# Convolution: image blocks folded about their middle, a transform in 64-row halves, and a last inverse step in 64x32 tiles

## The chip, the cores and the metric

The kernel runs on one core of a Trainium2 chip. A core has five engines: TensorE (PE) multiplies matrices, with a separate step that loads the stationary matrix (PEld); VectorE (DVE), ScalarE (ACT) and GpSimd (POOL) work element by element; SyncE (SP) only issues transfers. PE writes to PSUM, [...]results of PE are copied ("evicted") to SBUF by ACT or DVE. DMA engines move data between HBM and SBUF. Each engine works through its own queue in order. The metric is the device time of one launch in microseconds; smaller is better.

## The reference

The input is `x`, four images of 512x512 with 16 channels, fp32. Layer 0 adds to `x` a long 2-d convolution of its group-normalized form, with a filter given as a ratio of two polynomials, evaluated by FFT at twice the size. Layer 1 adds a 3x3 cosine-similarity convolution of the result, again normalized first. Cut to what matters here:

```python
H = jnp.fft.rfft2(h_truncated, s=(2 * l1, 2 * l2))
H_full = h0 + H[0]
X = jnp.fft.rfft2(x, s=(2 * l1, 2 * l2), axes=(-3, -2))
Y = jnp.einsum('...hwi,ijhw->...hwj', X, H_full)
y = jnp.fft.irfft2(Y, s=(2 * l1, 2 * l2), axes=(-3, -2))
return y[..., :l1, :l2, :]
...
x = x + _L0_conv_ref(_gn(x), L0_conv_h0, L0_conv_numerators, L0_conv_denumerator)
x = x + _L1_conv_ref(_gn(x), L1_conv_kernel, L1_conv_bias, L1_conv_radius)
```

The change is confined to layer 0.

## The kernel before

The program has four stages, one after the other. `filter_phase` makes the filter's transform along the width and stores its taps in `g_d`. `forward_phase` normalizes the images and transforms them along the width into `x_d`. `conv_phase` convolves along the height, one width frequency (a "row") at a time, into `y_d`. `last_phase` transforms back along the width (to `yw_d`) and does layer 1.

The work is written with a tile framework. A tile is taken from a pool with a fixed number of buffers, and waits for a free one. The framework orders the instructions of each engine itself when the program is built: what stands earlier in the program goes first, unless by its own estimate it isn't ready and something later is. So the order in the queues is fixed at build time, and is not always that of the text. `InOrder` forces the order only in `filter_phase`.

**forward_phase** runs over 4 images and 4 blocks of 128 image rows (`ht`). It loads four 1 MB pieces `xt` of a block (L626), folds the width about its middle into sums on DVE (`xu`, L632) and differences on POOL (L634), transposes both by PE through two PSUM tiles `pt` (L641), scales on the way out with ACT and DVE into `xw`, and multiplies with a fixed cosine and sine matrix `fwd` (L663). Each result `pf` (four PSUM tiles) is evicted to `xo`, the cosine half by DVE (L671), the sine half by ACT (L673), and `xo` is stored to `x_d` (L675).

**conv_phase** handles 513 rows: frequencies 1 to 511, and two planes for the two purely real ones. Height 512 is cut in 64 positions by 8 shifts; along the 64 a length-128 transform is taken. The work on a row is spread over several steps of the loop `step(n)`, each of which treats four rows at different depths, in four parts k = 0 to 3:

- `load_x`, `load_g`, `load_xe` are issued by SP at the start of a step.
- `turn_x` makes this row's transform matrix `dfs_n` out of a constant and its phase, one ACT and one DVE instruction.
- `x_part` (row n+2, at k=0, after `over_q`): one 128x128 by 128x256 matmul for each image (L766) into PSUM tiles `px` of two images each; each tile is evicted to `xe`.
- `x_late` (row n+2) on POOL: four products `xu` (L787), one product and one sum `xl` (L788, L789), and two stores to the scratch `xf_d`, from which `load_xe` fetches shifted copies a step later. `half_shift` copies the two remaining shifts inside SBUF by ACT (L798): one from `xe`, one from `xl`.
- `g_part` (row n+1): four matmuls of 64x128 pairs a part (L818, into `pg`), evicted to `gh` in two copies.
- `mix` (row n): 32 matmuls a part in four 128x32 column tiles (L834, into `pm`), evicted to `yf` in one copy.
- `over_q` (row n-1): four transposes a part (L855, into `pz`); ACT copies half of `pz` (`zq`, L862) and DVE works the rest through in five instructions (L863 to L867), using `pz` as scratch to the end. At the end POOL makes `zd` and folds `z` (L871, L873).
- `over_g` (row n-2, at k=2): eight matmuls of 128x64 by 128x256 in two column tiles (L892, into one tile `py`), one eviction to `yo`, one store to `y_d` by POOL's queue (L903).

The PSUM tiles of the loop are three `pg`, two `pm`, and three of the tag `full`, which `px`, `pz` and `py` share. The eviction helper `evict` counts: every third call goes to DVE (L716), the others to ACT (L718). A row makes 15 such calls. In the queues as built, ACT copies `xl` (second L798) ahead of the evictions `yf` and `gh` of k=2, though in the text it stands behind those of k=3.

A matmul in fp32 shows as two records in the profile, a transpose as one.

Of the kernel before, what the change touches and what calls it, by code (L numbers as in the profile page):

```python
# [69 lines left out]
def constants():  # L70
# [79 lines left out]
    f, sb = np.arange(F), np.arange(S)  # L150
    d = np.zeros((2, S, F, 2))
    co, si = turn(np.outer(sb + 31.5, f), F)
    d[0, :, :, 0], d[0, :, :, 1] = co, -si
    d[1, :, :, 0], d[1, :, :, 1] = si, co
    c["dfs"] = np.stack([d, np.stack([d[..., 1], -d[..., 0]], -1)], 2).reshape(P, -1)
# [5 lines left out]
    ig = np.zeros((32, 2, 2, 4, 2, 2, 2, 16))  # L161
    for s0 in range(4):
        for cx in range(2):
            for c2 in range(2):
                n = gg[:, None] * s0 + 4 * gg[:, None] * s1[None, :] + 32 * (cx + c2)
                co, si = turn(n, F)
                for b2 in range(2):
                    ig[:, cx, b2, s0, c2, 0, b2, :] = co / F
                    ig[:, cx, b2, s0, c2, 1, b2, :] = si / F
# [427 lines left out]
def forward_phase(tc, cst, x, mvs, x_d):  # L597
    nc = tc.nc
    with ExitStack() as ctx:
        cp = ctx.enter_context(tc.tile_pool(name="x_const", bufs=1))  # L600
        xp = ctx.enter_context(tc.tile_pool(name="x_in", bufs=8))
        sm = ctx.enter_context(tc.tile_pool(name="x_small", bufs=B))
        up = ctx.enter_context(tc.tile_pool(name="x_u", bufs=4))
        tp = ctx.enter_context(tc.tile_pool(name="x_t", bufs=2))
# [12 lines left out]

        for b in range(B):
            scale, bias = norm[b]
            twice = sm.tile([P, 8], F32, name="twice")  # L620
            nc.vector.tensor_add(twice, bias, bias)
            for ht in range(4):
                xt = []
                for w in range(4):
                    t = xp.tile([P, P, C], F32, name="xt")
                    nc.sync.dma_start(out=t, in_=x[b, ht * P : (ht + 1) * P, w * P : (w + 1) * P, :])  # L626
                    xt.append(t)

                su = []
                for w in range(2):  # L630
                    u = up.tile([P, P, C], F32, name="xu")
                    nc.vector.tensor_add(u, xt[w], xt[3 - w][:, ::-1, :])  # L632
                    su.append(u)
                    nc.gpsimd.tensor_sub(xt[w], xt[w], xt[3 - w][:, ::-1, :])  # L634
                halves = su + xt[:2]
                xw = tp.tile([P, 4, C, P], F32, name="xw")
                for i4 in range(4):
                    for w in range(4):
                        pt = ps_x.tile([P, 4, P], F32, name="pt")
                        for i in range(4):  # L640
                            nc.tensor.transpose(pt[:, i], halves[w][:, :, 4 * i4 + i], ident)  # L641
                        for i2 in range(2):
                            g = 2 * i4 + i2
                            dst = xw[:, w, 2 * g : 2 * g + 2, :]
                            src = pt[:, 2 * i2 : 2 * i2 + 2, :]
                            if i2 == 0 and w < 2:
                                nc.scalar.activation(dst, src, AF.Identity,
                                                     scale=scale[:, g : g + 1], bias=twice[:, g : g + 1])
                            elif i2 == 0:
                                nc.scalar.activation(dst, src, AF.Identity, scale=scale[:, g : g + 1])  # L650
                            elif w < 2:
                                nc.vector.tensor_scalar(dst, src, scale[:, g : g + 1],
                                                        twice[:, g : g + 1], ALU.mult, ALU.add)
                            else:
                                nc.vector.tensor_scalar(dst, src, scale[:, g : g + 1], None, ALU.mult)
                for rc in range(4):
                    o = op.tile([P, 2, 16, 8, C], F32, name="xo")
                    for c in range(2):
                        col = (2 * rc + c) * P
                        for i4 in range(4):  # L660
                            pf = ps_f.tile([P, 4, 16, 8], F32, name="pf")
                            for w in range(2):
                                nc.tensor.matmul(  # L663
                                    pf.rearrange("p i s t -> p (i s t)"), fwd[:, w, col : col + P],
                                    xw[:, 2 * c + w, 4 * i4 : 4 * i4 + 4, :].rearrange("p i h -> p (i h)"),
                                    start=(w == 0), stop=(w == 1),
                                )
                            dst = o[:, c, :, :, 4 * i4 : 4 * i4 + 4]
                            src = pf.rearrange("p i s t -> p s t i")[:, :, ::-1, :]
                            if c == 0:  # L670
                                nc.vector.tensor_copy(dst, src)  # L671
                            else:
                                nc.scalar.copy(dst, src)  # L673
                    for c in range(2):
                        nc.sync.dma_start(  # L675
                            out=dram(x_d[rc], None, c * X_ROW // 2 + (16 * ht * B + b) * C * 8,
                                     [B * C * 8, 16], [1, C * 8]),
                            in_=o[:, c].rearrange("p s t i -> p s (t i)"),
                        )
# [5 lines left out]
def conv_phase(tc, cst, g_d, x_d, y_d):  # L685
    nc = tc.nc
    with ExitStack() as ctx:
# [11 lines left out]
        dfs = load_const(nc, cp, cst, "dfs").rearrange("p (v n) -> p v n", v=2)  # L699
        dg = load_const(nc, cp, cst, "dg")  # L700
        ident = load_const(nc, cp, cst, "ident")
        ig = load_const(nc, cp, cst, "ig").rearrange("p (s c n) -> p s c n", s=4, c=2)
# [29 lines left out]
        def load_x(n):  # L732
            rc, r, plane = rows[n]
            x = io.tile([P, B, 8 * C], F32, name="x")
            t, w = x.rearrange("p b x -> p (b x)"), B * 8 * C
            if plane is None:
                nc.sync.dma_start(out=t, in_=dram(x_d[rc], r, 0, [w, P], [1, w]))
            else:
                nc.gpsimd.memset(t[S:], 0.0)
                nc.sync.dma_start(out=t[:S], in_=dram(x_d[rc], r, plane * S * w, [w, S], [1, w]))  # L740
            state["x", n] = x

        def turn_x(n):
# [8 lines left out]
            t = xlp.tile([P, 2 * F], F32, name="turn")  # L752
            nc.scalar.activation(t, dfs[:, 1], AF.Identity, scale=own[:, 1, at])
            m = xlp.tile([P, 2 * F], F32, name="dfs_n", bufs=2)
            nc.vector.scalar_tensor_tensor(m, dfs[:, 0], own[:, 0, at], t, ALU.mult, ALU.add)
            state["dfs", n] = m

        def x_part(n, b):

            if b == 0:  # L760

                state["xe", n] = xep.tile([P, 8, F, 2, 2, 2], F32, name="xe")
            if b % 2 == 0:
                state["px"] = ps_f.tile([P, 2, F, 2], F32, name="px", tag="full")
            px = state["px"]
            nc.tensor.matmul(px[:, b % 2].rearrange("p f c -> p (f c)"), state["x", n][:, b],  # L766
                             state["dfs", n], start=True, stop=True)
            if b % 2:
                evict(state["xe", n][:, 0, :, b // 2], px.rearrange("p k f c -> p f c k"))
            if b == B - 1:  # L770
                del state["x", n], state["dfs", n]

        def x_late(n):

            xe = state["xe", n][:, 0]
            fl = xe.rearrange("p f h c k -> p f (h c k)")
# [6 lines left out]
            xl = xlp.tile([P, F, 2, 2, 2], F32, name="xl")  # L783
            u = xlp.tile([P, F, 2, 2, 2], F32, name="xu")
            for c in range(2):
                for h in range(2):
                    nc.gpsimd.tensor_mul(u[:, :, h, c], xe[:, :, h, 1 - c], bc(late[:, 1 + c], 2, [P, F, 2]))  # L787
            nc.gpsimd.tensor_mul(xl.rearrange("p f h c k -> p f (h c k)"), fl, bc(late[:, 0], 2, [P, F, 8]))  # L788
            nc.gpsimd.tensor_add(xl.rearrange("p f h c k -> p (f h c k)"),  # L789
                                 xl.rearrange("p f h c k -> p (f h c k)"),  # L790
                                 u.rearrange("p f h c k -> p (f h c k)"))
            store(1, xl.rearrange("p f h c k -> p f (h c k)"))
            state["xl"] = xl

        def half_shift(n, half):

            dst, src = ((slice(0, 64), state["xe", n][64:, 0]), (slice(64, P), state["xl"][:64]))[half]
            nc.scalar.copy(state["xe", n][dst, 4].rearrange("p f h c k -> p (f h c k)"),  # L798
                           src.rearrange("p f h c k -> p (f h c k)"))
# [27 lines left out]
        def mix(n, g):  # L827
# [10 lines left out]
            if g == 7:  # L838

                state["y", n] = yp.tile([P, 16, 32, 4], F32, name="yf")  # L840
# [585 lines left out]
```

## Time and profile before

| | |
|---|---|
| median of 3 runs | 18402.83 us (18401.31 to 18431.59) |
| profiled execution, span from first to last instruction | 18387.3 us |
| mean granted TensorE clock | 0.957 |
| stage 1, `filter_phase` | about 0 to 5350 us |
| stage 2, `forward_phase` | about 5350 to 6460 us |
| stage 3, `conv_phase` | about 6460 to 15550 us |
| stage 4, `last_phase` | from about 15550 us |

Shares of the whole span: PE 90%, PEld 66%, DVE 63%, ACT 53%, POOL 57%. These are means over stages with different limits, so they say little about any one of them. In the groups of instructions, a line gives the source line, the engine, output and inputs, how often, then busy time and mean length, then the idle time of the engine just before and what ended it. PE's busy time is modelled: matmuls are pipelined, so groups of them overlap, and the distance from one group's start to the next is the better measure. "issue" as a releaser means that the engine waited for nothing that the profile shows.

### The profile page before, as it was taken

The numbers are of one execution on the slowest core, as the hardware profiler recorded it, in microseconds if no ns is written. First come the engines' busy times: TensorE is split into PE (matmuls) and PEld (weight loads), VectorE is DVE, ScalarE is ACT, GpSimd is POOL, SyncE is SP. The second block draws the span as 40 slices with busy tenths as digits, with TensorE's granted clock in tenths as the row PEclk, the third lists the DMA queues.
The fourth block names the chain that finished last, engine by engine and source line by source line (L and its number), as shares of the span: only waits on it lengthen the run. The fifth ranks groups of instructions, "written<-read, shape, count | busy, mean of one in ns | idle before, by whom it ended". The sixth has DMA issues, their size and how long they took to land. (4 is left out here: it accounts for less than half of the span.)

```text
span 18387.3 us, 530668 instructions
## 1 busy us (share of the span) xinstructions
PE 16516.6 (90%) x224908; PEld 12124.1 (66%) x224908; DVE 11547.2 (63%) x24155; ACT 9712.8 (53%) x18895; POOL 10465.0 (57%) x10653
## 2 busy tenths in 40 slices
PE   7899999999989988889888898888888887988898
PEld 4555555555544467777777777777777776877787
DVE  8988888888843345555555555555555554247887
ACT  5456666666632245555555555555555554106788
POOL 6456666666621066666666666666666664026776
PEclk8899999999999999999999999999999999998999
DMA  3665555555576588888888888888888887795431
GB/s 103 199 180 164 161 161 162 162 154 161 159 228 189 163 309 320 319 323 323 323 322 323 323 327 321 326 323 325 319 320 324 324 321 285 257 327 195 160 129 69
DMA packets 2918820, 4543.01 MB, mean 247 GB/s; under 512 B 117634, under 2 KB 2086492, under 8 KB 2809566
## 3 DMA queue, kind: packets, MB, share of 16 engines
q1 hardware_dynamic: 2686254, 3768.92, 60.5%
q0 software_dynamic: 174896, 605.89, 8.6%
q10 hardware_dynamic: 55296, 134.24, 2.2%
q8 instruction: 1772, 29.03, 0.6%
q14 instruction: 602, 4.93, 0.1%
HBM read 3031.24 MB, written 1477.31 MB: 245 GB/s over the span
## 5 line engine op out<-in xcount | busy, mean ns | idle before, releaser
L818 PE MATMUL pg<-c_dg,g 64*128 64x128 f32 x32832 | 2834.1, 291 | 336.6 <-ACT gh L718 172.3
L834 PE MATMUL pm<-xe,gh 128*32 128x64 f32 x131328 | 2395.9, 222 | 568.5 <-issue 326.8
L834 PEld LDWEIGHTS pm<-xe,gh 128*32 128x32 f32 x131328 | 2011.5, 110 | 1167.8 <-issue 980.5
L818 PEld LDWEIGHTS pg<-c_dg,g 64*128 64x128 f32 x32832 | 2284.3, 190 | 670.2 <-issue 256.1
L863 DVE TENSOR_TENSOR z<-zq,pz 128x256 f32<-128x256 f32 x2052 | 860.5, 419 | 2647.8 <-ACT zq L862 2567.5
L398 PE MATMUL pg<-c_dinv,sp 128*128 128x256 f32 x8192 | 2179.2, 414 | 223.9 <-ACT st L403 209.9
L398 PEld LDWEIGHTS pg<-c_dinv,sp 128*128 128x128 f32 x8192 | 1627.3, 204 | 915.5 <-ACT st L403 301.1
L716 DVE COPY gh<-pg 128x512 f32<-128x512 f32 x2046 | 1409.0, 689 | 1248.4 <-PE pg L818 1244.3
L378 POOL TENSOR_TENSOR x<-ab,ab 128x512 f32<-128x512 f32 x1024 | 1505.1, 1470 | 1039.3 <-ACT ab L361 993.9
L443 PE MATMUL pt<-ev_in,c_todd 128*128 128x512 f32 x4096 | 1992.3, 613 | 52.0 <-DMA ev_in<-g_d 26.6
L787 POOL TENSOR_TENSOR xu<-xe,c_late 128x256 f32<-128x256 f32 x2052 | 1390.9, 703 | 863.2 <-ACT xe L718 836.9
L376 DVE RECIPROCAL dn<-dn 128x256 f32<-128x256 f32 x1024 | 1781.1, 1739 | 0.0
L718 ACT COPY yf<-pm 128x512 f32<-128x512 f32 x2046 | 1210.2, 591 | 925.3 <-PE pm L834 910.9
L403 ACT COPY st<-pg 128x256 f32<-128x256 f32 x2048 | 1075.1, 625 | 1129.3 <-PE pg L398 724.4
L798 ACT COPY xe<-xl 64x1024 f32<-64x1024 f32 x513 | 538.4, 1050 | 1883.8 <-POOL xl L789 1883.8
L718 ACT COPY gh<-pg 128x512 f32<-128x512 f32 x2058 | 1199.9, 583 | 395.6 <-PE pg L818 386.7
L855 PE MATMUL pz<-c_ident,yf 128*128 128x128 f32 x8208 | 1371.6, 290 | 29.8 <-issue 15.0
L361 ACT COPY ab<-pab 128x512 f32<-128x512 f32 x2048 | 1121.6, 601 | 518.2 <-PE pab L352 282.0
L443 PEld LDWEIGHTS pt<-ev_in,c_todd 128*128 128x128 f32 x4096 | 810.0, 199 | 708.9 <-issue 531.9
L382 POOL TENSOR_TENSOR m<-m 128x256 f32<-128x256 f32 x1024 | 753.9, 736 | 885.8 <-DVE m L375 884.7
L789 POOL TENSOR_TENSOR xl<-xl,xu 128x1024 f32<-128x1024 f32 x513 | 1209.3, 2357 | 40.2
L1269 PE MATMUL pc<-l_band,xn 128*128 128x160 f32 (+2 forms) x6144 | 1079.4, 334 | 51.0 <-DVE e_o L1324 50.8
(205 smaller groups left out, 31650.4 us busy)
## 6 DMA issues: line engine op xcount, KB each, us to landing
xe<-xf_d SPq DMA_DIRECT2D x1026, 1536.0 KB, 10.1
g<-g_d SPq DMA_DIRECT2D x511, 1024.0 KB, 9.8
g_d<-st SPq DMA_DIRECT2D x64, 4096.0 KB, 25.7
ev_in<-g_d SPq DMA_DIRECT2D x1024, 256.0 KB, 4.8
g_d<-ot SPq DMA_DIRECT2D x1024, 256.0 KB, 2.6
xf_d<-xe POOLq DMA_DIRECT2D x513, 448.0 KB, 8.4
xf_d<-xl POOLq DMA_DIRECT2D x513, 448.0 KB, 5.4
x_d<-xo SPq DMA_DIRECT2D x128, 1024.0 KB, 5.1
```

The lines of the kernel that those rows point to most:

```text
L361: nc.scalar.copy(w["ab"][n], pp[n])
L376: nc.vector.reciprocal(w["dn"], w["dn"])
L378: nc.gpsimd.tensor_mul(w["x"], b, a[:, :, ::-1])
L398: nc.tensor.matmul(pg[:, k].rearrange("p a x -> p (a x)"), w["sp"][:, k, c, :], dinv[:, 2 * kp + k, c, :], start=(c == 0), stop=(c == 1),)
L443: nc.tensor.matmul(pt, todd[:, c, kc, hh * P : hh * P + P], ev[:, kc, c], start=(kc == 0), stop=(kc == 1),)
L716: nc.vector.tensor_copy(dst, src)
L718: nc.scalar.copy(dst, src)
L787: nc.gpsimd.tensor_mul(u[:, :, h, c], xe[:, :, h, 1 - c], bc(late[:, 1 + c], 2, [P, F, 2]))
L789: nc.gpsimd.tensor_add(xl.rearrange("p f h c k -> p (f h c k)"), xl.rearrange("p f h c k -> p (f h c k)"), u.rearrange("p f h c k -> p (f ...
L818: nc.tensor.matmul(pg[c][:, j % 4], g[half, j], dg[half], start=True, stop=True)
L834: nc.tensor.matmul(pm[32 * q : 32 * q + 32, g % 8], gh[:, f].rearrange("p c j -> p (c j)"), xe[:, :, f].rearrange("p t h c k -> p t (h c k ...
L855: nc.tensor.transpose(pz[:, t % 4].rearrange("p v q x -> p (v q x)"), y[:, at].rearrange("p g x -> p (g x)"), ident)
```

## The change

Three parts of the transform move.

**Folding the height.** In `forward_phase` a block of rows is now treated with its mirror image (`ht` with `3 - ht`). Both are loaded, folded in width, transposed and multiplied as before, the cosine part (`c = 0`) ahead of the sine part. The result of the mirrored block, read in reverse, is then added to and subtracted from that of the first: ACT copies one PSUM tile to `xa`, DVE adds and subtracts the other. The pools are recut: `x_in` 8 to 6 buffers, `x_u` 4 to 3, `x_t` 2 of 32 KB to 5 of 16 KB, and a new `x_a` with 4.

**The transform of a row.** Since sums and differences about the middle need only cosines or only sines, `x_part` multiplies two 64-row halves with a fixed matrix `dfs`, eight matmuls of 64x128 into two PSUM tiles, one for the real, one for the imaginary part. It no longer needs the row's phase, and is called ahead of `over_q`. The order of the elements in `xe`, `xl` and `yf` changes, and `xu` takes two products where it took four.

**The last inverse step.** The phase goes into the matrix of `over_g` instead (`turn_ig` in place of `turn_x`, with equal shapes). `over_g` does its sum in 16 matmuls of 64x32 by 64x256 into two tiles `py`, evicted by two calls to `evict`, so that a row has 16 calls. The store to `y_d` has runs of 1 KB where it had 2 KB; `last_phase` reads it in the new order in pieces of the same size.

```diff
-        xp = ctx.enter_context(tc.tile_pool(name="x_in", bufs=8))
+        xp = ctx.enter_context(tc.tile_pool(name="x_in", bufs=6))
...
+        def transform(xw, c, rc, i4):
+
+            col = (2 * rc + c) * P
+            pf = ps_f.tile([P, 4, 16, 8], F32, name="pf")
+            for w in range(2):
+                nc.tensor.matmul(
+                    pf.rearrange("p i s t -> p (i s t)"), fwd[:, w, col : col + P],
+                    xw[:, w, 4 * i4 : 4 * i4 + 4, :].rearrange("p i h -> p (i h)"),
+                    start=(w == 0), stop=(w == 1),
+                )
+            return pf.rearrange("p i s t -> p s t i")[:, :, ::-1, :]
...
+            for ht in range(2):
+                near, far = folded(b, ht), folded(b, 3 - ht)
+                for c in range(2):
+                    both = [turned(h[c], scale, (twice, None)[c]) for h in (near, far)]
+                    for rc in range(4):
+
+                        sums = [op.tile([P, 16, 8, C], F32, name=f"xo{k}") for k in range(2)]
                         for i4 in range(4):
...
+                            pa, pb = (transform(xw, c, rc, i4) for xw in both)
+                            pb = pb[:, ::-1]
+                            a = ap.tile([P, 16, 8, 4], F32, name="xa")
+                            nc.scalar.copy(a, pa)
+                            i = slice(4 * i4, 4 * i4 + 4)
+                            nc.vector.tensor_add(sums[0][:, :, :, i], a, pb)
+                            nc.vector.tensor_sub(sums[1][:, :, :, i], a, pb)
...
-            if b == 0:
-
-                state["xe", n] = xep.tile([P, 8, F, 2, 2, 2], F32, name="xe")
-            if b % 2 == 0:
-                state["px"] = ps_f.tile([P, 2, F, 2], F32, name="px", tag="full")
-            px = state["px"]
-            nc.tensor.matmul(px[:, b % 2].rearrange("p f c -> p (f c)"), state["x", n][:, b],
-                             state["dfs", n], start=True, stop=True)
-            if b % 2:
-                evict(state["xe", n][:, 0, :, b // 2], px.rearrange("p k f c -> p f c k"))
...
+            state["xe", n] = xep.tile([P, 8, F, B, 2], F32, name="xe")
+            px = [ps_f.tile([P, B, F], F32, name=f"px{c}", tag="full") for c in range(2)]
+            for b in range(B):
+                for c in range(2):
+                    half = slice(64 * c, 64 * c + 64)
+                    nc.tensor.matmul(px[c][:, b], state["x", n][half, b], dfs[half], start=True, stop=True)
+            for c in range(2):
+                evict(state["xe", n][:, 0, :, :, c], px[c].rearrange("p b f -> p f b"))
...
             for c in range(2):
-                for h in range(2):
-                    nc.gpsimd.tensor_mul(u[:, :, h, c], xe[:, :, h, 1 - c], bc(late[:, 1 + c], 2, [P, F, 2]))
...
+                nc.gpsimd.tensor_mul(u[:, :, :, c], xe[:, :, :, 1 - c], bc(late[:, 1 + c], 2, [P, F, B]))
...
-                state["py"] = ps_f.tile([P, 2, 2, 8, C], F32, name="py", tag="full")
...
+                state["py"] = [ps_f.tile([P, 2, 8, C], F32, name=f"py{h}", tag="full") for h in range(2)]
+            z, d, m = state["z", n], state["zd", n], state["ig", n]
+            c2 = k
+            for s0 in range(4):
...
-                nc.tensor.matmul(
-                    py[64 * half : 64 * half + 64, odd], ig[:, s0, c2],
-                    zs.rearrange("p (t h) j -> p h t j", h=2),
-                    start=(c2 == 0), stop=(c2 == 1),
-                )
...
+                for half in range(2):
+                    q = slice(64 * half, 64 * half + 64)
+                    nc.tensor.matmul(
+                        state["py"][half][32 * s0 : 32 * s0 + 32], m[q, s0, c2],
+                        zs[q].rearrange("p (t h) j -> p h t j", h=2), start=(c2 == 0), stop=(c2 == 1),
+                    )
...
-            evict(yo.rearrange("p (x j t) -> p x j t", x=4, j=C), py.rearrange("p o h t j -> p (o h) j t"))
...
+            for half in range(2):
+                evict(yo[:, half].rearrange("p (h j t) -> p h j t", h=2, j=C),
+                      state["py"][half].rearrange("p h t j -> p h j t"))
...
-                nc.gpsimd.dma_start(out=dram(y_d[rc], r, 0, [4 * P, P], [1, 4 * P]), in_=yo)
...
+                nc.gpsimd.dma_start(out=dram(y_d[rc], r, 0, [w, P], [P * w, 2], [1, w]), in_=yo)
...
+                if row(2) and k == 0:
+                    x_part(n + 2)
                 if row(-1):
                     for t in range(4):
                         over_q(n - 1, 4 * k + t)
                 if row(2) and k == 0:
-                    for m in range(B):
-                        x_part(n + 2, m)
                     x_late(n + 2)
                 if row(2) and k >= 2:
                     half_shift(n + 2, k - 2)
-                if row(3) and k == 2:
-                    turn_x(n + 3)
+                if row(-1) and k == 2:
+                    turn_ig(n - 1)
                 if row(-2) and k == 2:
-                    for m in range(4):
+                    for m in range(2):
                         over_g(n - 2, m)
```

## The prediction

> **What bounds the kernel now.** I read the page's slices first, then the busy times by stage, the waits of each engine in the longest stage, and the timeline of single rows there. Columns after the length: busy time of PE, PEld, DVE, ACT, POOL, then clock, DMA share, GB/s.
>
> ```profile
> 5378.00:6460.00 1082.00, 1026.27 (x3072) 511.55 (x3071) 398.72 (x543) 279.42 (x512) 152.48 (x36) 0.98 0.60 181
> 6600.00:15600.00 9000.00, 7994.17 (x182467) 6399.25 (x182456) 4877.85 (x13211) 4717.39 (x8610) 5696.92 (x5572) 0.98 0.86 321
> ```
>
> The first is the forward stage (PE busy 95%), the second the row loop of `conv_phase`. Its 513 rows start 17.64 us apart on average (first `px` matmul at 6466.1, last at 15499.2, over 512). No engine is full, so the loop is bound by waits:
>
> ```profile
> ACT xe L798 <- POOL xl L789: 1854.4, 504, 6.5
> ```
> ```profile
> PE pm L834 <- issue: 319.5, 321, 3.2
> PE pg L818 <- ACT gh L718: 160.3, 187, 3.7
> PE pg L818 <- issue: 157.3, 99, 3.7
> ```
>
> In nearly every row ACT stands 3.7 us in front of POOL's last `xl`. One row in order of time, PE, then POOL, then ACT:
>
> ```profile
> 12011.22 1.89 PE L766 MATMUL px<-dfs_n,x 128*128 128x256 f32 x8
> 12013.05 1.10 PE L834 MATMUL pm<-xe,gh 128*32 128x64 f32 x64
> 12022.74 0.42 PE L834 MATMUL pm<-xe,gh 128*32 128x64 f32 x14 [1.41 <-issue]
> 12023.10 1.16 PE L818 MATMUL pg<-c_dg,g 64*128 64x128 f32 x16
> 12028.13 1.89 PE L766 MATMUL px<-dfs_n,x 128*128 128x256 f32 x8
> ```
> ```profile
> 12012.95 1.36 POOL L787 TENSOR_TENSOR xu<-xe,c_late 128x256 f32<-128x256 f32 x2 [1.92 <-ACT xe L718]
> 12018.37 2.37 POOL L789 TENSOR_TENSOR xl<-xl,xu 128x1024 f32<-128x1024 f32 x1
> ```
> ```profile
> 12020.77 1.05 ACT L798 COPY xe<-xl 64x1024 f32<-64x1024 f32 x1 [3.74 <-POOL xl L789]
> 12021.84 0.58 ACT L718 COPY yf<-pm 128x512 f32<-128x512 f32 x1
> 12022.32 0.59 ACT L718 COPY gh<-pg 128x512 f32<-128x512 f32 x1
> ```
>
> The loop that sets the row: `px` starts at 12011.22; its first half is evicted; POOL does four `xu`, a store and two `xl`, to 12020.74 (9.5 us after `px`); ACT, which stood waiting with the k=2 evictions queued behind, copies `xl`, then evicts `yf` and `gh`; only then has PE a bank for the `pg` of k=3 (12023.10, 2.33 after the copy began); 5.03 us later comes the next `px`. Sum 16.9. Of 454 rows measured in the trace a tenth take under 16.90 us, half under 17.15. PE's own groups, start to start, are 4 x 1.03 (`pm`) + 3 x 1.09 + 1.08 + 0.42 (`pg`) + 4 x 0.58 (`pz`) + 1.83 (`px`) + 1.87 (`py`) = 14.9, so 2.0 us of each row is PE waiting. A long wait has a second price:
>
> ```profile
> 10014.94 0.60 PE L818 MATMUL pg<-c_dg,g 64*128 64x128 f32 x6 [2.96 <-issue]
> 10016.17 1.98 PE L892 MATMUL py<-z,c_ig 128*64 128x256 f32 x8
> ```
> ```profile
> 10015.00:10020.00 5.00, 5.00 (x57) 2.92 (x59) 2.18 (x6) 2.71 (x5) 0.57 (x1) 0.66 0.94 379
> ```
>
> After that pause the clock fell and the `py` group took 3.40 us instead of 1.87. Counting PE's pauses between 7000 and 15000 us: a half-rate spell followed 8 of 103 pauses of 1.5 to 2.0 us, 31 of 60 of 2.0 to 2.5, 19 of 27 of 2.5 to 3.0, and 10 of 12 of 3.0 to 3.5. There were 73 spells in 454 rows.
>
> [...]the spells in this trace are 3.41 us at 0.5[...]. [...]queue q8 moved 1772 packets, 29.03 MB, which is 16 KB each, and PE's pauses put down to "issue" fall where a block ends. Fetches are 3.3 us apart at the closest.
>
> **The change, part by part** (a row of the loop unless said).
>
> *x_part.* 4 matmuls of 128x256 (8 records) become 8 of 64x128 (16 records), exactly the form of a `pg` group: 1.83 to 1.09, saves 0.74.
>
> *over_g.* 8 matmuls (16 records) become 16 (32 records, 256 columns, 64x32). The old 16, two side by side, took 1.87. Eight side by side should take a quarter of the time per record, for twice the records: 0.86 plus the 0.2 that every group pays for the change of form: 1.07, saves 0.80. Bounds: no gain if only four run together; below 1.07 nothing is to be had. I take 1.07.
>
> PE's own work is thus 14.9 - 1.54 = 13.4. That is not the row: the loop above must be summed anew.
>
> *px to xl.* Both `px` tiles now end together, at +1.09, where half was ready at +0.9 before. ACT starts 0.2 later; the evictions (0.59 ACT, 0.69 DVE) end at +2.0, or at +2.4 in the third of rows in which both fall to ACT. POOL's four `xu` at 0.70 become two of 512 elements; nearest row `zd` L871, 1.27. So 2 x 1.27 + store 0.57 + 1.97 + 2.36 + gaps 0.2 = 7.65, and `xl` ends at +9.8 (9.5 before). If the new `xu` cost 1.47, like L378, +10.2.
>
> *xl to next px.* ACT's order is fixed at build time. I take it as it stands, copy first: 2.33 to `pg`. Then 5.03, less the 0.49 of the `pz` that now comes after `px`: 4.54.
>
> Loop: 9.8 + 0.03 + 2.33 + 4.54 = 16.7, against 16.9. Nearly the whole saving becomes waiting: 16.7 - 13.4 = 3.3 us, in one place, before `pg` of k=3. There the count above says 10 of 12. Instruction fetches may split the pause, so I take two of three. A spell costs about 1.6 us (`py` lost 1.53; 3.41 at half rate loses 1.7), and comes just before the 4.5 us of PE work that close the loop: +1.07. What rows take above the loop now is 17.64 - 16.9 = 0.74, of which spells are 73/454 x 1.6 = 0.26; the rest, 0.48, stays, with fetches up from 720 to 768 instructions a row: 0.5. Row: 16.7 + 1.07 + 0.5 = 18.27, +0.63; times 513, **+323 us**.
>
> *Evictions.* 15 a row become 16 (`yo` in two). Every third goes to DVE: with 15 the same ones in each row, never `yf`; with 16 the choice moves from row to row. Per row ACT gains about as much as it loses. Costed at nothing; within +-0.4 for rows in which `pg`'s two land on one engine.
>
> *y_d stores* in 1 KB runs instead of 2: 256 KB of 5.4 MB a row, on POOL's queue, after the loop's POOL work. POOL's issue is 0.58 now; up to 0.9 would hide behind its idle 2.4 us. *turn_ig* for *turn_x*: same shapes, same engines, nothing.
>
> *Forward stage.* Transposes and matmuls are as many. 256 DVE copies (0.688) become 256 ACT copies in place of ACT's old ones plus 512 DVE adds from PSUM; by L863 (256 elements, 0.419) some 0.69 each: DVE +177 us, to 575 of 1082, beside a PE that takes 3.4 us for each pair of tiles. Hidden; if not, at most +60. The first block needs 8 loads where 4 did, of which PE can start on half: +10. Range -15 to +60. *Last stage:* loads and matmuls of equal size: nothing.
>
> Sum: 18387.3 + 323 + 10 = 18720 span; 15.5 us lie around it (median 18402.8), so **18735**.
>
> **Rivals.** *PE is set free (faster).* If ACT's new order puts the `xl` copy behind the k=2 evictions, nothing gates `pg`; nobody else needs `xl` within the row. For it: `xl` comes 0.3 later and such orders are decided by small margins; against: `yf` of k=2 comes later too by the same `pz`. Then the row is 13.4 + fetch pauses, which rise from 1.04 (530 us of PE "issue" in 510 rows) to about 1.9, because 256 instructions pass in 13.4/3.0 = 4.5 us instead of 5.3, + 0.6 other waits = 15.9. DMA stands below it: 0.867 x 17.64 = 15.3. Time: -1.74 x 513 = 17510. *No spells.* Same loop, the pause split too finely for the clock: 16.7 + 0.5 + 0.2 = 17.4, so 18280. *A bank short (slower still).* `px` and `py` now take two of the three `full` banks at once, so `pz` of k=3 may wait for the DVE chain of `pz` k=2, which starts behind ACT's copy: 0.7 more a row, 19080. It decides once that chain ends later than copy + 3.4 us; it ended at +4.05 in the row shown. *Tiles not side by side.* `py` stays 1.9: the pause is 2.5, spells less frequent, about 18550.
>
> **How the numbers follow.** Forecast 0.42, bank short 0.10, tiles 0.08: slower 0.60. PE free 0.25, no spells 0.15 (half of it within the bound). A difference of 0.2% (37 us) is what a measurement can tell here. Faster 0.33, same 0.07, slower 0.60. The likeliest case's own range is 18450 to 18950; with PE free and the missing bank taken in, 17500 to 19050.
>
> **What would show it.** Right: `px` groups at 1.09, `py` near 1.07, `pg` waiting for ACT in most rows, PEclk near 0.9 in the loop. Wrong: PE's share above 93% in the loop with ACT's wait for `xl` gone, or a `py` group at 1.9.

## The result and the profile after

The changed kernel takes 18739.43 us (median of 4 runs, 18719.5 to 18758.74) against 18402.51 us (4 runs, 18401.31 to 18431.59): the ratio is 1.0175, 95% interval 1.0162 to 1.0189. The forecast was 18735. In the profiled executions the span went from 18387.3 to 18757.0 us, 369.7 more. The first and last `px` matmul cut both spans into the same pieces:

| piece | before, us | after, us | difference |
|---|---|---|---|
| start to the first transpose of the forward stage | 5377.8 | 5390.9 | +13 |
| forward stage, to the first `px` | 1088.3 | 1132.8 | +44.5 |
| 512 rows, first `px` to last | 9033 (17.643 a row) | 9321 (18.205 a row) | +288 |
| last `px` to the end | 2888 | 2912 | +25 |

The first piece runs unchanged code. The last holds the end of the last rows and the last stage, which reads `y_d` in another order. Over all executions profiled below the first piece takes 5371 to 5391 us in either kernel; the last takes 2874 to 2888 in the kernels with the code of before and 2886 to 2912 in the changed ones, 2881 and 2893 on average. So some 12 of these 37 us may belong to the change, and the rest is scatter. Nearly all that the change did lies in the forward stage and in the rows.

The busy time by stage, with the columns as in the prediction (length, then PE, PEld, DVE, ACT, POOL, clock, DMA share, GB/s):

```profile
5390.00:6523.00 1133.00, 1038.65 (x3072) 520.46 (x3072) 538.57 (x800) 276.76 (x512) 157.75 (x40) 0.97 0.58 174
6600.00:15600.00 9000.00, 7370.24 (x189311) 5975.98 (x189299) 4753.24 (x12984) 4683.99 (x8709) 5421.73 (x4440) 0.93 0.84 312
```

In the loop PE is busy for less of the time (7994 before, 7370 now), its clock fell from 0.98 to 0.93, and no other engine and no transfer is busier. So PE waits more. For what, the table of PE's waits in the loop tells (total us, times, longest); the next line is ACT's largest wait:

```profile
PE pm L845 <- issue: 1079.2, 611, 4.1
PE pg L829 <- issue: 178.8, 120, 3.2
PE pm L845 <- ACT gh L730: 90.1, 109, 2.5
PE pg L829 <- ACT gh L730: 58.6, 127, 1.1
```
```profile
ACT xe L809 <- POOL xl L800: 1146.7, 442, 5.7
```

"issue" at `pm` was 319.5 us in 321 pauses before. Waits for ACT are less than a seventh of it, and ACT itself waits less for `xl` than before (1854.4). One row in PE's timeline:

```profile
12016.30 0.41 PE L904 MATMUL py<-zd,ig_n 64*32 64x256 f32 x2
...
12017.32 0.31 PE L845 MATMUL pm<-xe,gh 128*32 128x64 f32 x5
12019.64 1.08 PE L845 MATMUL pm<-xe,gh 128*32 128x64 f32 x59 [2.01 <-issue]
12020.65 1.16 PE L829 MATMUL pg<-c_dg,g 64*128 64x128 f32 x16
...
12029.81 0.49 PE L829 MATMUL pg<-c_dg,g 64*128 64x128 f32 x4 [1.25 <-issue]
```

`py` now takes 1.02 us from its start at 12016.30 to the next `pm`, and `px` 1.09. But PE stops after 5 of the 64 matmul records of a `mix` group, in the middle of work that had begun, and again within a `pg` group, and the profile shows nothing that it waits for. In the row before it came after 8 records, in the next after 3, as a boundary after a fixed number of instructions would drift. From the first stop to the second there are 255 matmul records, each with a weight load, so 510 instructions. At 12017.18, some 0.45 us before the first stop, a 16 KB packet of queue q8, which carries the instructions, starts and takes 0.88 us; PE goes on 1.6 us after its end. The next two packets start at 12021.10 and 12027.60, and PE goes on 2.2 us after the start of the second. The queue's line (packets, MB, share):

```profile
q8 instruction: 1870, 30.64, 0.6%
```

The same holds for all of these stops. Between 7000 and 14500 us there are 612 of more than 0.5 us, and from each to the next the number of matmul records is a whole multiple of 127 to 128, in all 611 cases to within one record. In 98% of them PE goes on between 2.15 and 2.55 us after the start of a q8 packet (median 2.35; in the kernel before, 312 stops, the same). So PE stops where a block of 254 to 256 instructions ends, the content of one packet (768 a row over 3.02 packets; 720 over 2.83 before). That the packet of the next block starts too late is the reading of these times.

Of the prediction's sum this gives, each a row and from the trace between 7000 and 14500 us: PE's own groups 14.9 before and 13.4 after; waits of PE 1.86 and 3.28; time at half clock 0.61 and 2.45, of which about half is lost (an estimate from the granted clock of 0.5). That is -1.5, +1.4 and up to +0.9, where +0.56 was measured. PE is idle in only 3% of the time at half clock, so it is not that the slow time falls into the pauses; where the difference of 0.25 lies stays open.

### The profile page after: what moved, and what is told of

It is laid out like the page before. It is cut to its first block, busy times and chain, and to the rows that moved or that the text cites. A ratio compares the mean times of both kernels' runs of the same rounds, so it can differ in the third digit from the quotient of the medians.

```text
span 18757.0 us, 556552 instructions
## 1 busy us (share of the span) xinstructions
PE 16125.6 (86%) x237220; PEld 11887.0 (63%) x237220; DVE 11701.0 (62%) x24582; ACT 9803.2 (52%) x19237; POOL 10335.4 (55%) x9633
## 5 line engine op out<-in xcount | busy, mean ns | idle before, releaser
L845 PE MATMUL pm<-xe,gh 128*32 128x64 f32 x131328 | 2593.5, 229 | 1216.8 <-issue 1116.1
L845 PEld LDWEIGHTS pm<-xe,gh 128*32 128x32 f32 x131328 | 2142.8, 115 | 1815.7 <-issue 1640.2
L829 PE MATMUL pg<-c_dg,g 64*128 64x128 f32 x32832 | 2957.4, 306 | 266.8 <-issue 188.1
L829 PEld LDWEIGHTS pg<-c_dg,g 64*128 64x128 f32 x32832 | 2385.1, 203 | 621.9 <-issue 335.5
L730 ACT COPY gh<-pg 128x512 f32<-128x512 f32 x2736 | 1535.1, 587 | 1173.9 <-PE pg L829 1153.5
L728 DVE COPY gh<-pg 128x512 f32<-128x512 f32 x1368 | 945.4, 691 | 1303.3 <-PE pg L829 1293.5
L917 POOL DMA_DIRECT2D y_d<-yo x511 | 398.2, 779 | 2192.2 <-issue 1316.1
L798 POOL TENSOR_TENSOR xu<-xe,c_late 128x512 f32<-128x512 f32 x1026 | 1164.4, 1135 | 310.1 <-ACT xe L730 236.0
L730 ACT COPY yf<-pm 128x512 f32<-128x512 f32 x1368 | 819.3, 599 | 816.1 <-PE pm L845 808.4
L881 POOL TENSOR_TENSOR zd<-z 128x512 f32<-128x512 f32 x513 | 650.9, 1269 | 957.7 <-DVE z L873 957.3
```

The source lines that it names most:

```text
L798: nc.gpsimd.tensor_mul(u[:, :, :, c], xe[:, :, :, 1 - c], bc(late[:, 1 + c], 2, [P, F, B]))
L829: nc.tensor.matmul(pg[c][:, j % 4], g[half, j], dg[half], start=True, stop=True)
L845: nc.tensor.matmul(pm[32 * q : 32 * q + 32, g % 8].rearrange("p m c -> p (m c)"), gh[:, f].rearrange("p c j -> p (c j)"), xe[:, :, f].rear ...
```

## The experiments

Two theories of what holds the changed row at 18.2 us. L, the prediction's: the loop from `px` through POOL's `xl` and ACT's copy to `gh` and the `pg` of k=3; pauses for instructions stand only where PE would wait anyhow. F: PE's instructions come in blocks of 254 to 256, too late, and the pauses and the half clock after them hold the row. All figures a row below are from the traces between 7000 and 14500 us; "instr." is PE's idle time put down to issue, "others" its idle time put down to anything else, "half clock" the time at a granted clock of 0.5, "blocks" the packets of q8.

| kernel | ratio to before, interval | row | instr. | others | half clock | blocks |
|---|---|---|---|---|---|---|
| before | 1 | 17.64 | 1.04 | 0.82 | 0.61 | 2.83 |
| b_pool_copy2 | 1.0003 (0.9996 to 1.0010) | 17.69 | 1.28 | 0.61 | 1.19 | 2.83 |
| b_split | 1.0106 (1.0091 to 1.0121) | 17.99 | 1.75 | 0.34 | 0.76 | 3.02 |
| after | 1.0175 (1.0162 to 1.0189) | 18.20 | 2.88 | 0.40 | 2.45 | 3.02 |
| a_old_py2 | 1.0100 (1.0085 to 1.0115) | 17.88 | 2.05 | 0.49 | 1.67 | 2.89 |
| a_pool_copy | 1.0118 (1.0101 to 1.0136) | 18.02 | 3.10 | 0.13 | 2.35 | 3.01 |
| a_half_mix | 1.0325 (1.0310 to 1.0341) | 18.70 | 0.01 | 2.96 | 4.48 | 2.01 |
| a_pool_half_mix2 | 0.9897 (0.9880 to 0.9913) | 17.19 | 0.17 | 2.63 | 3.47 | 2.01 |
| a_g4 | 1.0151 (1.0134 to 1.0168) | 18.04 | 1.99 | 1.04 | 2.58 | 3.01 |
| a_pool_g4 | 0.9892 (0.9877 to 0.9906) | 17.14 | 2.43 | 0.11 | 1.82 | 3.02 |
| a_pool_half_mix_g4 | 0.9497 (0.9481 to 0.9513) | 15.70 | 0.11 | 1.50 | 1.89 | 2.02 |

### The loop through ACT taken away

```diff
-            nc.scalar.copy(state["xe", n][dst, 4]..., src...)
+            (nc.scalar.copy, nc.gpsimd.tensor_copy)[half](state["xe", n][dst, 4]..., src...)
```

> The changed kernel with the copy of xl into xe (second half_shift) on POOL instead of ACT, so that ACT no longer stands in front of POOL's xl with evictions queued behind it. Theory L (the loop px, POOL's xl, ACT's copy and gh eviction, pg of k=3 sets the row, and the pauses at PE's instruction blocks only stand where PE would wait anyway): the row falls from 18.2 us to 16.0 to 17.3, total 17500 to 18250. Theory F (PE's own pauses for instructions, 2.9 us a row, and the half-clock spells after them set the row): row 18.0 to 18.4, total 18600 to 18850, PE's issue pauses still over 2.5 us a row.

Measured: 18596.33 us, row 18.02. ACT's wait for `xl` is gone, and this is PE's largest wait in the loop:

```profile
PE pm L845 <- issue: 1197.2, 681, 4.6
```

The row fell by 0.18, not by 1 to 2: the pauses for instructions grew from 2.88 to 3.10 and kept the row where it was. L alone is refuted.

### A third of PE's instructions taken away

```diff
-            for q in range(4):
+            for q in range(4) if g % 2 == 0 else ():
...
-                    pm[32 * q : 32 * q + 32, g % 8]..., gh[:, f]..., xe[:, :, f]...
+                    pm[32 * q : 32 * q + 32, g % 8 : g % 8 + 2]..., gh[:, f]..., xe[:, :, f : f + 2]...
```

> The changed kernel with the 128 mix matmuls of 64 columns a row replaced by 64 of 128 columns (each takes two frequencies with the weights of the first, so half of the products by gh are left out): as many columns stream, with 512 PE instructions a row instead of 768, two blocks of 256 instead of three. Theory F: issue pauses fall from 2.9 us a row to under 1.2, hardly any half-clock spells, row 15.0 to 16.4 us, total 17100 to 17850. Theory L: the loop of 16.7 us stays, without spells: row 16.9 to 17.4, total 18050 to 18350.

Measured: 18982.15 us, row 18.70: slower than the changed kernel, though the pauses for instructions fell to nothing, and outside what both theories gave. F alone is refuted too. PE's waits now:

```profile
PE pz L866 <- DVE z L878: 573.5, 320, 4.3
PE pg L829 <- ACT gh L730: 536.3, 558, 3.1
PE pm L845 <- ACT gh L730: 313.8, 160, 2.0
PE pg L829 <- issue: 3.5, 5, 0.9
```

These are the prediction's waits, for ACT and for the bank behind the DVE chain. One of them in ACT's timeline and then in PE's:

```profile
12024.44 1.04 ACT L809 COPY xe<-xl 64x1024 f32<-64x1024 f32 x1 [4.10 <-POOL xl L800]
12025.51 0.59 ACT L730 COPY yf<-pm 128x512 f32<-128x512 f32 x1
12025.99 0.59 ACT L730 COPY gh<-pg 128x512 f32<-128x512 f32 x1
```
```profile
12026.64 1.16 PE L829 MATMUL pg<-c_dg,g 64*128 64x128 f32 x14 [1.57 <-ACT gh L730]
12028.63 0.67 PE L866 MATMUL pz<-c_ident,yf 128*128 128x128 f32 x4 [0.84 <-DVE z L878]
...
12030.68 1.93 PE L845 MATMUL pm<-xe,gh 128*32 128x128 f32 x32
```

The copy waits 4.10 us for `xl`, the evictions follow it, and only then comes `pg`; the clock then halves (the last line: 1.93 us for a group that takes 1.08 at full clock). With all waiting in this place, 4.48 us of each row run at half clock, more than in any other kernel of the table. Loop plus half clock is thus a bound of its own, at 18.70. The loop itself is as long as the prediction summed it: no row of this kernel takes under 16.59 us, and the 13 rows without any half clock take 16.59 to 16.64.

### Both taken away

Theory D was formed here: two bounds lie side by side, and removing one uncovers the other. The edit is both of the above.

> Both edits in one: the changed kernel with the xl copy on POOL and with 64 mix matmuls of 128 columns a row (half of the products by gh left out, 512 PE instructions a row). Each alone left the row at 18.0 and 18.7 us. Theory D (two bounds lie side by side: the POOL/ACT loop with the half-clock spells of its one long pause, and PE's own instruction pauses with theirs; removing one uncovers the other): row 14.6 to 16.2 us, total 16900 to 17700, issue pauses under 0.3 us a row, spells under 100 between 7000 and 15000 us. If a third thing holds the row (data transfers, DVE, the evictions): row 17 or more, total over 18100.

Measured: 18207.25 us, row 17.19. Faster than either edit alone, which supports D, but not the 14.6 to 16.2 expected from two bounds alone: the other case that was written down, a third bound at 17 or more, came in. Waits for ACT and for instructions have shrunk to 0.09 and 0.17 us a row, and this has come up:

```profile
PE pm L845 <- DMA xe<-xf_d: 1160.8, 269, 6.6
```

### Undoing the last inverse step

```diff
-                for half in range(2):
-                    q = slice(64 * half, 64 * half + 64)
-                    nc.tensor.matmul(
-                        state["py"][half][32 * s0 : 32 * s0 + 32], m[q, s0, c2], zs[q]..., ...)
+                half, odd = s0 // 2, s0 % 2
+                nc.tensor.matmul(
+                    state["py"][odd][64 * half : 64 * half + 64], m[:, s0]..., zs..., ...)
```

> The changed kernel with the old form of the last inverse step, for its time alone: 8 matmuls of 128x64 a row instead of 16 of 64x32 (the weights are ig's by another reading, so the sums of the two columns are left out), 736 PE instructions a row instead of 768; py takes about 1.9 us a row instead of 1.0. If PE's work set the row: 19.05, total 19190. Theory D: what py saves is given back as waiting, so undoing it costs little: row 18.0 to 18.4, total 18650 to 18850, issue pauses down from 2.9 to 2.0-2.5 us a row.

Measured: 18577.05 us, row 17.88; `py` takes 1.88 us again. The lower total is below even theory D's range: with 0.86 us of PE work put back, the row became 0.32 shorter. The pauses for instructions fell by 0.83 and the time at half clock by 0.78. In this kernel the 64x32 tiles cost more than they saved. The sum -0.83 for the pauses, half of -0.78 for the clock, +0.86 for PE's work and +0.09 for other waits gives -0.27, so their 32 more instructions a row, and less time to fetch them in, account for most of it.

### The number of instructions alone

```diff
-            nc.tensor.matmul(px[:, b % 2]..., state["x", n][:, b], state["dfs", n], ...)
+            for h in range(2):
+                nc.tensor.matmul(px[:, b % 2, 64 * h : 64 * h + 64]..., state["x", n][:, b],
+                                 state["dfs", n][:, 128 * h : 128 * h + 128], ...)
```

The eight `py` matmuls were cut in the same way, and stand in another order within their group.

> The kernel before with every px and py matmul cut into two column halves: the same multiplications, ACT/POOL loop and traffic, but 768 PE instructions a row instead of 720, as many as the changed kernel has. Theory F: PE's issue pauses rise from 1.0 us a row to 1.5 or more and bring more half-clock spells; row 18.1 to 18.6 us, total 18600 to 18900. Theory L: only PE's own extra time counts (0 to 0.3 us a row) where it isn't hidden: total 18380 to 18550.

Measured: 18575.66 us, row 17.99, between the two ranges. The groups themselves grew by 0.08 us (`px` 1.82 to 1.88, `py` 1.88 to 1.90), the pauses for instructions by 0.71, while waits for others fell by 0.48. So 48 more instructions a row slow the kernel before by some 0.3 us a row, without any of the change's other effects.

The table can be read for one more thing. PE's own groups (14.9 us before, 15.0 in b_split, 14.2 in a_old_py2, 13.4 after and in a_pool_copy) and the pauses for instructions, divided by the blocks of a row, give 5.63, 5.55, 5.62, 5.39 and 5.47 us for a block. So under this traffic, what the work of a block lacks to about 5.5 us is filled up with pauses on average. In a_half_mix a block holds 6.6 us of work, and there are no pauses. The 5.5 is not the spacing of the blocks: they come 5.96 to 6.23 us apart (row divided by blocks), since other waits and the half clock add to it. That it acts as a floor is a reading of these sums.

### Less to transfer

```diff
+            if n % 4:
+                state["g", n] = state["g_kept"]
+                return
             g = io.tile([P, C, 8 * C], F32, name="g")
+            state["g_kept"] = g
```

> The changed kernel with g loaded in every fourth row only (the other rows use the tile again, three quarters of g left out): some 0.8 MB of 5.4 MB a row less on the DMA engines, all else as it was. If the fetch of PE's instructions is slow because it stands behind the data transfers: issue pauses fall from 2.9 to 2.0-2.5 us a row, row 17.3 to 17.9, total 18250 to 18600. If its latency doesn't depend on traffic, or theory L holds: total 18680 to 18780.

> The changed kernel with the xl copy on POOL and g loaded in every fourth row only (three quarters of g left out): no loop through ACT, and 0.8 MB of 5.4 MB a row less to move; PE's instructions as they are. Theory T (instruction blocks come late because they stand behind the data, and the data itself is the third bound): issue pauses 2.0 to 2.5 us a row instead of 3.2, row 16.5 to 17.4 us, total 17850 to 18300. If the lateness of a block doesn't depend on the data: issue pauses 3.0 or more, row 17.8 to 18.1, total 18500 to 18650.

> All three in one: the xl copy on POOL, 64 mix matmuls of 128 columns a row, g loaded in every fourth row (half of the products by gh and three quarters of g left out). Theory T (three bounds, transfers the lowest with 17.2 us a row): PE's waits for DMA nearly vanish and the row comes near PE's own 13.4: 13.6 to 15.2 us, total 16400 to 17250. If the wait for xe is set by the chain of store and load rather than by the volume moved: row 16.7 to 17.2, total 17950 to 18250, with PE's long waits for xe still there.

Measured, by the trace's count with 4.9 MB a row instead of 5.7: 18649.34 us (row 18.04), 18178.1 (17.14) and 17448.74 (15.70). In the first, the pauses for instructions fell as theory F had it (2.88 to 1.99), but the row hardly moved, and the total lies between the two ranges: waits for ACT and DVE rose from 0.39 to 1.04, as L has it. Without the loop the same edit is worth 0.88 us a row (18.02 to 17.14), within the range expected. With all three edits the row comes to 15.70, above the 13.6 to 15.2 expected, and the waits for `xe` halve (all DMA waits 2.50 to 1.25 us a row) but do not vanish. How much of them is volume, and how much the chain of store and load from one step to the next, stays open.

### The kernel before without its loop

The copy of `xl` on POOL, in the kernel before.

> The kernel before with its xl copy on POOL. PE's own work there is 14.9 us a row and its issue pauses 1.0. Theory D: the loop of 16.9 us is gone, the issue pauses grow as the row becomes shorter (to 1.5 to 2.0 us) and few spells remain: row 16.6 to 17.3, total 17900 to 18250, less than both kernels. If the loop was never what held the row before: 18330 to 18430.

Measured: 18416.26 us (20 runs) against 18410.08 (23 runs), no change. The waits for ACT were 0.43 us a row and are gone; waits for DMA rose from 0.21 to 0.51, those for instructions from 1.04 to 1.28, and the time at half clock doubled. The loop of 16.9 us that the prediction put at the head of the kernel before is real: no row there takes under 16.87 us, and half take under 17.16. With the copy on POOL a tenth take under 16.1, but others take longer (a tenth over 19.9, against 19.2), and the mean stays. The loop was one of three bounds of about the same height, and taking it away alone brings nothing.

### The forward stage

```diff
                             nc.vector.tensor_add(sums[0][:, :, :, i], a, pb)
-                            nc.vector.tensor_sub(sums[1][:, :, :, i], a, pb)
```

> The changed kernel without the 256 subtractions of the forward stage (the second sums are left out, the first ones are stored twice), so that DVE has 354 us there instead of 530. If DVE's bursts hold PE in the forward stage: its length from the first transpose to the first px falls from 1133 to 1095-1115 us. If the 44 us come from the doubled loads in front of each block pair and from the end of the stage: 1125 to 1135. Rows 18.1 to 18.3.

Measured, in one run: the stage takes 1131.7 us, against 1132.8 to 1136.0 in the nine profiles that have it whole. PE's waits in the changed stage, from 5380 to 6520 us, in the changed kernel:

```profile
PE pt L637 <- DVE xw L648: 31.1, 22, 2.8
PE pf L659 <- DVE xo L684: 21.2, 7, 3.8
PE pt L637 <- DVE xw L651: 18.7, 24, 0.9
PE pt L637 <- DVE xu L625: 16.0, 4, 8.4
```

Of the 44.5 us that the stage gained, PE's idle time makes 32 (62 before, 94 now) and its busy time 12; the time at half clock rose from 44 to 71 us, half of which is about the latter. The largest new wait is the second line, 21.2 us: PE stands seven times for DVE's additions, the first time because a folding `xu` of 2.29 us, held up by its load, stands ahead of them on DVE. The kernel before has no wait of `pf`. The fourth is the start, at which PE waits for the second block (8.4 us at once). The first and third are the pairs of transposes at the turn from one half to the next, where up to 24 transposes now follow one another with no `pf` between them (12 before); they are hardly new, 49.8 us against 45.3 before.

Without the subtractions the second line fell to 14.0 us and all of PE's idle time to 84, but the time at half clock rose to 91 us and gave it back. So the unchanged length of the stage does not tell that the subtractions are hidden: some 7 us of waiting go with them. Why the clock was lower without them stays open.

### A version that loads less

The runs pointed to less traffic and no loop through ACT. Two kernels make one of the six loaded copies of `xe` (t=2) on the chip, in four copies of 32 rows, with the `xl` copy on POOL:

```diff
+        def quarter_shift(n, k):
+            src = state["xe", n][32 * k + 32 : 32 * k + 64, 0] if k < 3 else state["xl"][:32]
+            copy = (nc.scalar.copy, nc.vector.tensor_copy, nc.vector.tensor_copy, nc.gpsimd.tensor_copy)[k]
+            copy(state["xe", n][32 * k : 32 * k + 32, 2]..., src...)
...
-            for t in (1, 5):
+            for t, by in ((1, 2), (5, 1)):
```

> The kernel before with the xl copy on POOL, and the third of xe's eight shifted copies (t=2) made on the chip from xe and xl in four copies of 32 rows (one on ACT, two on DVE, one on POOL) instead of loaded: 0.5 MB of 5.4 MB a row less to move. Theory T (the transfers stand behind both the waits for xe and the late instruction blocks): row 17.0 to 17.5 us instead of 17.7, total 18080 to 18330, faster than both kernels. If the four copies (about 1.05 us each) get in the way of evictions by as much: total 18380 to 18700.

> The changed kernel with the same two edits. Theory T: issue pauses 2.6 to 2.9 us a row instead of 3.2, row 17.3 to 17.8 us instead of 18.0, total 18220 to 18500: still not under the kernel before with the same edits, since PE has 768 instructions a row. If the copies get in the way by as much as the traffic gives: total 18550 to 18800.

Measured: 21206.01 us on the kernel before (ratio 1.153, 1.1513 to 1.1547) and 18773.21 on the changed one (1.0207, 1.0190 to 1.0225). The first misses by far. The second misses the range of theory T by 270 us and falls into the other, for copies that get in the way: its pauses for instructions fell to 1.85 us a row, further than T gave, but PE waits 1.19 us for DVE. The groups of the first, from 7000 to 15000 us (busy time, mean ns):

```profile
L804 DVE COPY xe<-xe 32x1024 f32<-32x1024 f32 x689 | 2341.6, 3399 | 15.4
...
L789 POOL TENSOR_TENSOR xl<-xl,xu 128x1024 f32<-128x1024 f32 x344 | 918.4, 2670 | 27.0
...
L804 ACT COPY xe<-xe 32x1024 f32<-32x1024 f32 x345 | 360.6, 1045 | 445.8 <-DVE xe L716 445.8
```

The copy that takes 1.05 us on ACT takes 3.40 on DVE, and POOL's `xl` beside it 2.67 instead of 2.37. Two such copies in a row put 6.8 us ahead of DVE's `gh`, and PE waits 4.65 us a row for DVE. In the changed kernel the DVE copy takes 2.29 us on average. It took longer beside POOL's work. Two pairs from the first kernel's timeline, the first beside POOL's `xl` (its two lines follow) with 6.82 us, the second while POOL works on nothing with 1.39:

```profile
7055.77 6.82 DVE L804 COPY xe<-xe 32x1024 f32<-32x1024 f32 x2
7057.33 1.96 POOL L788 TENSOR_TENSOR xl<-xe,c_late 128x1024 f32<-128x1024 f32 x1
7059.37 2.67 POOL L789 TENSOR_TENSOR xl<-xl,xu 128x1024 f32<-128x1024 f32 x1
...
7240.77 1.39 DVE L804 COPY xe<-xe 32x1024 f32<-32x1024 f32 x2
```

Such undisturbed copies are rare, 7 of 689 here and 8 of 874 in the changed kernel, but all 15 took 0.68 or 0.69 us. With the copies on ACT or POOL the idea was not tried; no kernel that computes the whole reference beat the kernel before.

## Why the prediction was right, and where it was not

*The total.* 18735 against 18739.43. The rows brought +288 where +323 was forecast, the forward stage +44.5 where +10 was, and the other 37 us of the difference of the profiled spans are scatter for the most part. That the total came out within 5 us is luck: two errors of 35 us cancel, and the rows' term came about in another way than forecast.

*px and py.* Right: 1.09 and 1.02 us, forecast 1.09 and 1.07, so `py` came out 0.05 under what was called its bound. That eight 64x32 tiles work side by side was the author's estimate, and the times agree with it: a record of 256 columns took 0.229 us as 128x128 (`px` before, 8 in 1.83), 0.117 as 128x64 (`py` before, 16 in 1.87) and 0.032 as 64x32 (32 in 1.02). PE's own work is 13.4 us as forecast.

*The saving turns into waiting.* Right in size, wrong in kind. The loop came out at what was summed: 16.7 was forecast, and the shortest rows of the changed kernel take 16.62. But the middle row takes 17.77, so something else holds most rows. Forecast were 3.3 us of waiting in one place, before `pg` of k=3, for ACT's `gh`, with fetches a small 0.5 beside it. Measured are 3.28 us in all, of which 2.88 are pauses for instructions, at block ends that move through the row, and 0.32 are waits for ACT. The step that failed is "Nearly the whole saving becomes waiting ... in one place"; the wait that it names does come, in nearly that size and with the half clock after it, but only in the kernel in which the pauses for instructions are gone (a_half_mix). Of the signs that were named in advance, `px`, `py` and the clock (0.93) came, and `pg` waiting for ACT in most rows did not: there are 127 such waits in 494 rows.

*Half-clock spells.* Two rows of three forecast, 0.61 a row measured (267 in 439 rows, 7000 to 15000 us). The number is right, but not for the reason given. They follow shorter pauses than the forecast's single one: 49% of 225 pauses of 2.0 to 2.5 us and 61% of 148 of 2.5 to 3.0, counted from the start of one matmul record to the start of the next. By the trace they come after steps of 3.41 us in which PE is idle for some 2.0 us (the last section has the count).

*The rival "PE is set free".* It was given 0.25 and 15.9 us a row. a_pool_copy is that case, and its row is 18.02. The mis-sized term is the fetch: about 1.9 us a row was worked out from "256 instructions pass in 4.5 us", 3.10 was measured. Left out of that sum was the half clock, 2.35 us a row, of which about half is lost. The floor of 15.3 us for DMA was too low too: a_pool_half_mix2 still waits for `xe` at 17.2, with transfers busy 89% of the time. "A bank short" (a bank is one PSUM buffer of the loop) was the right guess for one wait (`pz` behind the DVE chain, 1.2 us a row in a_half_mix), which the changed kernel hardly shows (0.07).

*The forward stage.* The range of -15 to +60 held, the value of +10 did not. The additions that were doubted are not wholly hidden: PE waits 21.2 us for them. The start was priced at +10; PE's waits for loaded and folded blocks there are 10.6 us in the stage, 6.0 before. The slower clock, some 12 us, was not priced. The evictions (16 instead of 15 calls) and the shorter runs of the `y_d` stores were put at nothing, and no run tested them alone.

*Fetches.* In this loop the pauses for instructions come to 1.04 us a row before and 2.88 after. Only in the kernels with two blocks in a row of the loop, of 6.6 us of work each, do they nearly vanish (0.01 to 0.17).

## What to carry to other kernels

On a kernel with many small matmuls and busy transfers, count PE's instructions as a resource of its own: a tile shape that halves the time and doubles the instructions can lose, as the 64x32 tiles did here (taking them back gave 0.32 us a row). When several bounds lie within a microsecond, test a cause by removing it alone and together with its neighbours; here each of two removals alone made little or made it worse, and three together, in a kernel that leaves out work, gave 5%. Waiting on PE had a second price in the half clock (0.61 us a row before, 2.45 after), so a shorter stage in front of an unmoved wait can come out slower.

## What the runs showed of the hardware

- PE stopped where a block of 254 to 256 of its instructions ended: in the changed kernel all 611 distances between stops were whole multiples of 127 to 128 matmuls with their weight loads, to within one. It went on 2.35 us (2.2 to 2.5 in nine of ten) after a 16 KB packet of q8 began. In the loops whose transfers are busy 84 to 87% of the time, work and pauses of a block came to 5.4 to 5.6 us together; with 0.8 MB a row less to move, to 5.1 and 5.2.
- The half-clock spells of the two traces, 285 before and 524 after, begin within 12 ns on one grid of 3413 ns in each, and 186 and 382 of them last 3413 ns, the shortest length. Take the steps of this grid that ran at full clock between 7000 and 15000 us, and add up PE's idle time in each (gaps over 0.06 us). In the changed kernel all 148 steps with 2.0 us or more were followed by half clock, 77 of 84 with 1.8 to 2.0, 28 of 84 with 1.6 to 1.8, and 12 of 1715 with less; in the kernel before, all 41 with 2.0 or more and 1 of 2173 with less than 1.6. So 2.0 us of idle time in one step was followed by a spell in every case. A pause that is split over two steps leaves less in each, and of the pauses of 2.0 to 2.5 us in the changed kernel 49% were followed by one. In the kernel with one long wait a row PE ran at half rate for 4.48 of 18.70 us.
- A copy from SBUF to SBUF of 32x1024 fp32 took 1.05 us on ACT and 1.04 on POOL. On DVE it took 0.68 to 0.69 us in the 15 cases in which POOL worked on nothing, and 3.40 and 2.29 us on average beside POOL, whose own sum took 2.67 there and 2.37 in the kernel before. What makes the two slower side by side was not shown.
